# Layer 0's end, layer 1's degrees and layer 2's gates: part of the dilation moved, and two products put in column groups

## The chip, the core and the metric

The kernel runs on one core of one Trainium2 chip, in one launch. The metric is the device time of that launch in microseconds. TensorE multiplies matrices and writes to PSUM, VectorE and ScalarE do element-wise work and empty PSUM, GpSimd (POOL) computes a few powers and issues the stores to DRAM, SyncE (SP) issues the loads.

## The reference, cut to what matters

Four graph layers follow each other on `x` (16 x 1024 x 128, f32) with an adjacency matrix `adj` (16 x 1024 x 1024, zeros and ones) per batch. After each layer, `x = layernorm(x + layer(x))`.

Layer 0 is an attention: `h = x W^T + b`, `e = h A h^T` made symmetric, masked by `adj`, softmax along the rows, `h' = relu(att h)`, and one gate `c = sigmoid([x, h'] g)` that mixes `x` and `h'`.

Layer 1 first thins out the adjacency ("dilation"): row by row, every neighbour whose rank is a multiple of half the row's count is removed, from the row and from the column of the same number, and the next row sees what is left:

```python
sf = jnp.where(num > T_DIL, (num + K_DIL - 1) // K_DIL, 1)
rank = jnp.cumsum(nbi)
rm = row & (rank % sf == 0)
carry = carry.at[n].set(row & keep)
carry = carry.at[:, n].set(carry[:, n] & keep)
```

Then come three steps of `agg = (adj_d @ x) / deg; out = agg @ Wr + x @ Wx + b`, normed per row, relu and batch norm, where `deg` is the row sum of the thinned adjacency. Their outputs are joined and multiplied by `Wl`.

Layer 2 is an attention as in layer 0 with three gates in place of one: `i, f, o = sigmoid([x, h'] w)`, result `o * tanh(sigmoid(i h' + f x))`. Layer 3 is two graph convolutions with the normed adjacency.

## The kernel before, in words

A batch's adjacency is 1024 x 1024; it is kept as fp8 in SBUF (`Y[b]`, 8 tiles of 128 rows), four batches to one tile `Yq`. The phases are one after the other, each with its own pools: layer 0, the dilation, layer 1 (three steps over all batches), layers 2 and 3 together.

**Order of the work.** Each phase is written as Python generators, one per batch and stage, that `take_turns` (L803) runs round-robin: one stretch of each up to its `yield`. `in_turn` (L807) does it for the attention layers: while batch b is in `attention`, batch b+1 is in `before` and batch b-1 in `after`; at the end, the last `attention` runs with the last but one `after`, and then the last `after` (L825). This gives the order of the program. The build then places the instructions on each engine's queue; mostly in that order, but an instruction whose inputs, tile and PSUM bank are ready may be put ahead of one that comes earlier in the program. [...]

**Layer 0** (L884 to L995). `before` loads `adj` and turns it (L922), `attention` has eight stages of e (L723), mask and maximum (L958), exponent (L962) and product with h (L969). `after` takes relu, the gate, the mixture and the layer norm (`normed`, with a power on POOL, L744), and stores `x1` (L992). The gate goes through `gates` (L768 to L781), which holds the 32 gate columns as the stationary operand and puts the four quarters of the 1024 nodes into four column groups of TensorE:

```python
nc.tensor.matmul(p[32 * q:32 * q + 32, :], g, x[:, q * N // 4:(q + 1) * N // 4], ..., tile_position=(0, 32 * q))
```

ScalarE copies the result (L776), and two transposes (L779) turn it back. The PSUM pool `ps_h` of the layer has two banks, tag "h".

**Dilation** (L1002 to L1181). It works on blocks of 128 rows (k = 0 to 7) and two groups of eight batches (g), 16 steps in all. `prepare` (L1019) counts on TensorE (L1054, matmuls of 128 columns or one column) and puts counts and thresholds together on VectorE, for four batches at a time. `fixed_point` (L1069) evaluates six times which of the block's own entries are removed: `mid` on VectorE (L1085), eight one-column matmuls `pd` (L1088), then `ti` (L1092). `removal` (L1121) forms the ranks of a batch's rows (L1131, L1133), the kept entries (L1135) and the thinned rows and columns. Before the change, the phase begins with `prepare` of both groups, then the inverse roots of the degrees (L1169 to L1175), and then a loop: `fixed_point` of step i in turn with the removals of step i-1, after each of which `prepare` of step i+1 begins. The first pass of the loop has `fixed_point` alone.

**Layer 1, first step** (L1255 to L1378, L1352 on). For batch b, `first` computes the degrees: `degree_product` (L1255) multiplies the thinned adjacency with a 128 x 128 block of twos, 2 x 8 matmuls of 512 columns, of whose 128 equal rows one is used. ScalarE copies that row (L1357), a small transfer makes it 8 x 128 (L1359), VectorE takes the minimum and the inverse (L1360 to L1363), it goes to DRAM (L1364) and comes back to all partitions (L1349). Then follow the transposes of x (L758), and the product with the adjacency as two f32r parts, `hi` and `lo` (L1251, L1252, `lo` with one buffer), 64 matmuls of 512 columns (L1284). `out` (L1388 to L1404) multiplies with Wx and Wr, `keep` transposes, stores, and forms the product for the next step. The three are in turn for batches b+1, b and b-1. The order of the batches is 8 to 15, then 0 to 7; the thinned adjacency of the latter is loaded from DRAM (L1331).

**Layers 2 and 3** (L1455 on). `before` joins layer 1's outputs (L765) and prepares the attention; `attention` is as in layer 0 (L723, L1571 to L1590); `after` takes relu, the gates (L1596 to L1605), the mixture, norm, and the whole of layer 3, with its propagations (L1527). Its PSUM pool `ps_h` has two banks too. The gates before the change are, for each of eight blocks of nodes, two f32 matmuls with the nodes as the stationary operand and three moving columns (L1600, L1601).

Of the kernel before, what the change touches and what calls it, by code (L numbers as in the profile page):

```python
# [22 lines left out]
P = 128  # L23
# [5 lines left out]
GB = 8  # L29
# [610 lines left out]
def fast_kernel(ctx: ExitStack, tc: tile.TileContext, t: dict, out: bass.AP, flag: bass.AP):  # L640
# [166 lines left out]
    def in_turn(before, attention, after, ahead=1, state=None):  # L807
# [17 lines left out]
        take_turns([beside, after(state[B - 1], B - 1)])  # L825
# [55 lines left out]

    with ExitStack() as ph:

        early = ph.enter_context(tc.tile_pool(name="l0_early", bufs=1, reuse_waits="tile"))  # L884
# [110 lines left out]
        in_turn(before, attention, after)  # L995

    with ExitStack() as ph:
        sb = ph.enter_context(tc.tile_pool(name="dl_sb", bufs=2, reuse_waits="tile"))
        small = ph.enter_context(tc.tile_pool(name="dl_small", bufs=3, reuse_waits="tile"))
        ps_b = ph.enter_context(tc.tile_pool(name="dl_pb", bufs=2, space=PSUM, reuse_waits="tile"))
        ps_d = ph.enter_context(tc.tile_pool(name="dl_pd", bufs=1, space=PSUM, reuse_waits="tile"))
        ps_s = ph.enter_context(tc.tile_pool(name="dl_ps", bufs=3, space=PSUM, reuse_waits="tile"))  # L1010
        ps_c = ph.enter_context(tc.tile_pool(name="dl_pc", bufs=2, space=PSUM, reuse_waits="tile"))

        def words(v):
            return v.bitcast(I32)

        def per_member(v):
            return v[:, :, None].to_broadcast([P, v.shape[1], P])

        def prepare(st, k, g):  # L1019

            ks = slice(k * P, (k + 1) * P)
            st.with_last = k >= NT - 2
            st.sk = sb.tile([P, GB, P], F16, name="sk")
            st.v1m = small.tile([P, GB], F32, name="v1m")
            st.l1 = small.tile([P, GB], F32, name="l1")

            st.front = sb.tile([P, GB, P], BF16, name="front", bufs=3)
            if st.with_last:
                st.last = sb.tile([P, GB, P], FP8, name="last")
            for q in range(GB // QB):  # L1030
                qs = slice(q * QB, q * QB + QB)
                b0 = g * GB + q * QB
                gs = slice(b0, b0 + QB)
                Yg = Yq[b0 // QB]
                uY = sb.tile([P, QB, P], FP8, name="uY")
                nc.vector.tensor_tensor(words(uY), words(Yg[:, :, k, ks]),
                                        words(upper8)[:, None, :].to_broadcast([P, QB, P // 4]), op=OP.bitwise_and)
                front = st.front[:, qs, :]
                kf = [kb for kb in range(4) if kb != k]
                nc.vector.tensor_tensor(front, Yg[:, :, kf[0], ks], Yg[:, :, kf[1], ks], op=OP.add)  # L1040
                if k < 4:
                    nc.vector.tensor_tensor(front, front, Yg[:, :, kf[2], ks], op=OP.add)
                else:
                    back = sb.tile([P, QB, P], BF16, name="back")
                    nc.vector.tensor_tensor(back, Yg[:, :, kf[2], ks], Yg[:, :, kf[3], ks], op=OP.add)
                    nc.vector.tensor_tensor(front, front, back, op=OP.add)
                s0 = ps_b.tile([P, QB, P], F32, name="s0")
                for i in range(QB):
                    terms = [(Y[b0 + i][:, kb, ks], P if kb <= k else 1, step0 if kb == k else None)
                             for kb in range(4 if k >= 4 else 0, NT)]  # L1050
                    if k >= 4:
                        terms.insert(0, (front[:, i, :], P, None))
                    for j, (y, n, m) in enumerate(terms):
                        nc.tensor.matmul(s0[:, i, :n], y, twos[:, :n] if m is None else m,  # L1054
                                         start=(j == 0), stop=(j == len(terms) - 1))
                l1 = st.l1[:, qs]
                nc.vector.tensor_tensor(st.sk[:, qs, :], s0, uY, op=OP.mult)
                nc.vector.tensor_scalar(st.v1m[:, qs], s0[:, :, 0], 0.5, -1.0, op0=OP.mult, op1=OP.add)
                nc.vector.tensor_scalar(l1, s0[:, :, 0], -1.0, None, op0=OP.add)
                if not st.with_last:  # L1060

                    nc.vector.tensor_tensor(past[:, k, gs], l1, s0[:, :, P - 1], op=OP.subtract)
                nc.vector.tensor_add(st.v1m[:, qs], st.v1m[:, qs], off[:, k, gs])
                nc.vector.tensor_add(l1, l1, off[:, k, gs])
                if st.with_last:
                    nc.vector.tensor_tensor(st.last[:, qs, :], st.sk[:, qs, :], per_member(l1), op=OP.is_equal, saturate=False)
                yield

        def fixed_point(st, k, g):  # L1069

            ks = slice(k * P, (k + 1) * P)
# [90 lines left out]
        for s in steps[:G2]:  # L1162
            for _ in prepare(*s):
                pass
# [543 lines left out]
```

## Time and profile before

| what | us |
|---|---|
| three timed runs | 3050.39, 3050.43, 3054.73 |
| the profiled run, span of the core | 3049.5 |
| TensorE busy | 2825.3 (93%) |
| VectorE busy | 2325.2 (76%) |
| ScalarE busy | 2018.8 (66%) |
| L1261, degrees: 256 matmuls, one | 0.380 |
| L1600 and L1601, gates: 512 records, one | 0.252 |
| L774, layer 0's gates: 256 records, one | 0.391 |

Busy time of TensorE is modelled from the records, and matmuls overlap, so that the mean of one is more than what a stream of them takes per matmul; the distance between starts is the better measure. An f32 matmul has two records.

By stages: layer 0 lasts to about 725 us, the dilation to 1145, layer 1's first step to about 1540, its other two to about 1850, and layers 2 and 3 to the end. Granted clock, where a stretch shows it, is the share of TensorE's full clock.

### The profile page before, as it was taken

Reading aid. Unit: us, or ns where it says so; the run is one execution under the profiler, and the core shown is the slowest. Engines: PE = TensorE matmul, PEld = TensorE weight load, DVE = VectorE, ACT = ScalarE, POOL = GpSimd, SP = SyncE. Lnnn points to the kernel's source line nnn. Section 1 sums busy time; section 2 is a strip of 40 time slices with the busy share of each in tenths; the row PEclk is TensorE's granted clock in tenths of the full one; section 3 lists DMA queues with packets and bytes.
Section 4 is the critical chain, followed back from the end, with each engine's and each line's share of the span. In section 5 each row is a group of like instructions: output and inputs, shape, how many; then the busy total and the mean of one; then the engine's idle time right before and its main releaser. Section 6 shows DMA issues by size and latency. Waiting matters only on the chain.

```text
span 3049.5 us, 42855 instructions
## 1 busy us (share of the span) xinstructions
PE 2825.3 (93%) x15187; PEld 1794.2 (59%) x15250; DVE 2325.2 (76%) x5972; ACT 2018.8 (66%) x3425; POOL 315.2 (10%) x292
## 2 busy tenths in 40 slices
PE   7999999996999989999999987999999999999995
PEld 3444444443666657777788873556555555555554
DVE  7898889887999986666678785676766776777665
ACT  5877787773888886655555435666666666666653
POOL 0000000003000001111122231000000000000000
PEclk9999999997999999999999998999999999999997
DMA  5344344430000043223367692011112211111000
GB/s 162 131 159 152 132 138 159 152 118 29 2 2 2 2 158 107 88 91 120 122 231 251 227 336 76 35 63 59 66 57 71 73 57 56 56 56 56 21 14 22
DMA packets 123217, 297.97 MB, mean 98 GB/s; under 512 B 12656, under 2 KB 64624, under 8 KB 115824
## 3 DMA queue, kind: packets, MB, share of 16 engines
q1 hardware_dynamic: 102384, 211.13, 20.6%
q0 software_dynamic: 20608, 84.00, 7.7%
q8 instruction: 122, 2.00, 0.3%
q14 instruction: 103, 0.84, 0.1%
HBM read 211.04 MB, written 84.02 MB: 97 GB/s over the span
## 4 chain that ended last, share of the span: by engine, by line
PE 58%; DVE 21%; ACT 9%; DMA 5%; issue 5%; POOL 3%; SPq 0%; POOLq 0%; ACTq 0%; DVEq 0%
PE acc L1284 9%; PE pmm L723 8%; PE ph L1527 7%; PE acc L1590 6%; PE ph L765 6%; PE ph L758 4%; PE ph L1388 4%; DMA an<-in_adj 3%; ACT xn L798 3%; PE s L1131 2%; PE acc L969 2%; POOL ln_rstd L744 2%; PE ph L1513 2%; DVE mid L1085 2%; DVE ln_st L791 2%
## 5 line engine op out<-in xcount | busy, mean ns | idle before, releaser
L723 PE MATMUL pmm<-G,hT 128*128 128x512 f32 x1024 | 520.2, 630 | 1.9 <-DVE mx L1576 1.4
L723 PEld LDWEIGHTS pmm<-G,hT 128*128 128x128 f32 x1024 | 188.3, 201 | 174.2 <-issue 148.7
L798 ACT ACTIVATE xn<-xn,ln_nb,ln_rstd 128x128 f32<-128x128 f32 x512 | 206.6, 481 | 91.9 <-DVE ln_nb L796 91.9
L1590 PE MATMUL acc<-em,hs 128*128 128x512 f32 x512 | 256.0, 612 | 12.1 <-DVE hs L1587 10.5
L969 PE MATMUL acc<-em,hs 128*128 128x512 f32 x512 | 243.5, 599 | 18.2 <-DVE hs L966 16.8
L1284 PE MATMUL acc<-a,hi 128*128 128x512 f32 x768 | 242.0, 400 | 1.1 <-ACT hi L1251 0.9
L1284 PE MATMUL acc<-a,lo 128*128 128x512 f32 x768 | 241.2, 398 | 1.9 <-DVE lo L1252 1.9
L744 POOL TENSOR_TENSOR ln_rstd<-ln_rstd,mhalf 128x8 f32<-128x8 f32 x64 | 105.4, 1646 | 1324.2 <-DVE ln_rstd L741 1266.2
L1133 ACT ACTIVATE q<-s,negc 128x512 f16<-128x512 f32 x256 | 170.3, 696 | 58.2 <-DVE negc L1112 22.3
L915 ACT ACTIVATE ab<-an 128x1024 bf16<-128x1024 f32 x128 | 134.5, 1052 | 105.8 <-DMA an<-in_adj 66.6
L1131 PE MATMUL s<-step,carry 128*128 128x384 bf16 (+3 forms) x1034 | 197.6, 302 | 7.3 <-DVE carry L1101 3.2
L1576 DVE CUSTOM_DVE_ANT_0 em<-pmm,msk 128x1024 f32<-128x1024 f32 x128 | 156.0, 1219 | 54.7 <-PE pmm L723 51.9
L1145 ACT ACTIVATE carry<-pc,negone 128x512 fp8e4<-128x512 f32 x256 | 166.5, 698 | 35.7 <-PE pc L1144 26.3
L958 DVE CUSTOM_DVE_ANT_0 em<-pmm,msk 128x1024 f32<-128x1024 f32 x128 | 156.1, 1219 | 35.0 <-PE acc L969 30.5
L1571 ACT ACTIVATE msk<-A,nbig 128x1024 bf16<-128x1024 fp8e4 x128 | 146.0, 1141 | 50.2 <-DVE mx L1576 48.4
L1284 PEld LDWEIGHTS acc<-a,lo 128*128 128x128 f32 x768 | 142.9, 188 | 42.8 <-DVE lo L1252 9.5
L918 DVE SCALAR_TENSOR_TENSOR chk<-an 128x1024 fp8e4<-128x1024 f32 x128 | 156.3, 1221 | 14.0 <-DMA an<-in_adj 13.6
L1284 PEld LDWEIGHTS acc<-a,hi 128*128 128x128 f32 x768 | 141.7, 188 | 34.0 <-ACT hi L1251 1.4
L923 DVE TENSOR_SCALAR carry<-pt 128x1024 fp8e4<-128x1024 bf16 x128 | 155.7, 1217 | 6.2 <-PE pt L922 6.1
L969 PEld LDWEIGHTS acc<-em,hs 128*128 128x128 f32 x512 | 90.9, 190 | 113.9 <-issue 87.7
L1388 PE MATMUL ph<-Wx,hT 128*128 128x128 f32 x768 | 152.3, 281 | 4.9 <-DVE l2WT L709 3.2
L962 ACT ACTIVATE em<-em,nmx 128x1024 f32<-128x1024 f32 x128 | 146.9, 1147 | 12.3 <-DVE nmx L960 11.8
(285 smaller groups left out, 6448.6 us busy)
## 6 DMA issues: line engine op xcount, KB each, us to landing
an<-in_adj SPq DMA_DIRECT2D x128, 512.0 KB, 3.9
adj_d<-carry POOLq DMA_DIRECT2D x16, 1024.0 KB, 4.9
A<-dil_d SPq DMA_DIRECT2D x16, 1024.0 KB, 6.6
rdeg<-rdeg_d SPq DMA_DIRECT2D x32, 512.0 KB, 4.2
ag_d<-ag POOLq DMA_DIRECT2D x32, 512.0 KB, 5.5
ag<-ag_d SPq DMA_DIRECT2D x32, 512.0 KB, 6.3
A<-adj_d SPq DMA_DIRECT2D x16, 1024.0 KB, 4.8
xn<-in_x SPq DMA_DIRECT2D x16, 512.0 KB, 4.0
```

The source lines that it names most:

```text
L723: nc.tensor.matmul(p[:, h * 512:(h + 1) * 512], lhsT, rhs[:, h * 512:(h + 1) * 512], start=True, stop=True)
L744: nc.gpsimd.tensor_tensor(r, r, mhalf[:, :n], op=OP.pow)
L765: nc.tensor.matmul(p, W, x[:, c], start=(i == 0), stop=(i == len(pairs) - 1))
L798: nc.scalar.activation(r[:, i, :], r[:, i, :], AF.Identity, scale=rstd[:, i:i + 1], bias=nb[:, i:i + 1])
L969: nc.tensor.matmul(s.acc[:, c], hs, em[:, c], start=(jt == 0), stop=(jt == NT - 1))
L1131: nc.tensor.matmul(s[:, lo or 0:], y, twos if lo is None else step[:, :512 - lo], start=(j == 0), stop=(j == len(terms) - 1))
L1133: nc.scalar.activation(q[:, h * 512:(h + 1) * 512], s, AF.Abs, bias=st.negc[:, i:i + 1])
L1145: nc.scalar.activation(Y[b][:, hb, ks], pc, AF.Relu, bias=negone, saturate=False)
L1284: nc.tensor.matmul(acc, part[:, jt, :], pieces[h * NT // 2 + i][:, j, :], start=(jt == 0 and p == 0), stop=(jt == NT - 1 and p == 1))
L1388: nc.tensor.matmul(p[:, i * P:(i + 1) * P], x[:, j * P:(j + 1) * P], W, start=(n == 0), stop=(n == 1))
L1527: nc.tensor.matmul(p, part[:, jt, :], A[:, jt, c], start=(jt == 0 and i == 0), stop=(jt == NT - 1 and i == 1))
L1590: nc.tensor.matmul(s.acc[:, c], hs, em[:, c], start=(jt == 0), stop=(jt == NT - 1))
```

## The change

Three things are changed.

*The first counts.* `prepare`, `fixed_point`, `removal` and `removals` move out of the dilation's block to before layer 0, with their pools held in an object `dl`. Their lines are otherwise unchanged, except that PSUM tags come from `dl.tags`. `in_turn` takes one more stream, `tail`, that comes first in turn with the end of the last batches. Layer 0 passes `first_counts`: `prepare` and `fixed_point` of step 0. It closes the pool of layer 0's early tiles, which now lie on the right side of SBUF, and opens the dilation's pools for counts there; its PSUM is layer 0's `ps_h`, tag "h". The dilation's own block begins with `prepare` of step 1, and its loop with i = 1.

*The degrees.* `degree_product` has 32 matmuls with 32 columns of twos, each over a quarter of the nodes (256 columns), in four column groups of one PSUM bank; the row is copied in four pieces.

*The gates of layer 2.* They go through `gates`, with weights padded with zeros to 32 columns.

```diff
-        take_turns([beside, after(state[B - 1], B - 1)])
+        take_turns([iter(tail), beside, after(state[B - 1], B - 1)])
...
+    def first_counts(psum):
+        early_ctx.close()
+        dl.counts = dl.ctx.enter_context(tc.tile_pool(name="dl_counts", bufs=2, side="right", reuse_waits="tile"))
+        dl.small = dl.ctx.enter_context(tc.tile_pool(name="dl_small", bufs=3, side="right", reuse_waits="tile"))
+        dl.ps_b = dl.ps_d = psum
+        dl.tags = "h", "h"
+        yield from prepare(*steps[0])
+        yield from fixed_point(*steps[0])
...
-        early = ph.enter_context(tc.tile_pool(name="l0_early", bufs=1, reuse_waits="tile"))
+        early_ctx = ExitStack()
+        early = early_ctx.enter_context(tc.tile_pool(name="l0_early", bufs=1, side="right", reuse_waits="tile"))
...
-        in_turn(before, attention, after)
+        in_turn(before, attention, after, tail=first_counts(ps_h))
...
-        for s in steps[:G2]:
-            for _ in prepare(*s):
-                pass
+        for _ in prepare(*steps[1]):
+            pass
...
-        for i in range(len(steps) + 1):
+        for i in range(1, len(steps) + 1):
             streams = [fixed_point(*steps[i])] if i < len(steps) else []
-            if i:
-                streams.append(removals(steps[i - 1], steps[i - 1 + G2] if i - 1 + G2 < len(steps) else None))
+            streams.append(removals(steps[i - 1], steps[i - 1 + G2] if i - 1 + G2 < len(steps) else None))
...
-            self.gw = wts.tile([P, 2, 3], F32, name="l2gw")
+            self.gw = wts.tile([P, 2, 32], F32, name="l2gw")
+            nc.vector.memset(self.gw, 0.0)
...
-            for h in range(H2):
-                c = slice(h * 512, (h + 1) * 512)
-                acc = ps_a.tile([P, 512], F32, name="acc")
-                for jt in range(NT):
-                    nc.tensor.matmul(acc, twos[:, :P], A[:, jt, c], start=(jt == 0), stop=(jt == NT - 1))
-                yield acc, c
+            acc = ps_a.tile([P, 512], F32, name="acc")
+            for jt in range(NT):
+                for q in range(4):
+                    nc.tensor.matmul(acc[32 * q:32 * q + 32, :N // 4], twos[:, :32], A[:, jt, q * N // 4:(q + 1) * N // 4],
+                                     start=(jt == 0), stop=(jt == NT - 1), tile_position=(0, 32 * q))
+            for q in range(4):
+                yield acc[32 * q:32 * q + 1, :N // 4], slice(q * N // 4, (q + 1) * N // 4)
...
-                    nc.scalar.copy(row[:, c], acc[0:1, :])
+                    nc.scalar.copy(row[:, c], acc)
...
-            pg = ps_h.tile([P, NT, 3], F32, name="pg", tag="h")
-            for i in range(NT):
-                c = slice(i * P, (i + 1) * P)
-                nc.tensor.matmul(pg[:, i, :], s.xT[:, c], gw[:, 0, :], start=True, stop=False)
-                nc.tensor.matmul(pg[:, i, :], hpT[:, c], gw[:, 1, :], start=False, stop=True)
+            pg = gates(ps_h, wide("x3T")[:, :N // 4], (gw[:, 0, :], s.xT), (gw[:, 1, :], hpT))
             gt = small.tile([P, NT, 3], F32, name="gt")
-            nc.vector.tensor_add(gt, pg, gb[:, None, :].to_broadcast([P, NT, 3]))
+            nc.vector.tensor_add(gt.rearrange("p (q t) g -> p q t g", t=2), pg[:, :, :, :3],
+                                 gb[:, None, None, :].to_broadcast([P, 4, 2, 3]))
```

## The prediction

> **What bounds the kernel now.** I read the page's busy shares first (TensorE 93%, VectorE 76%, ScalarE 66%), then the chain that ended last in the three places that the change touches, then busy time by stretch there.
>
> In layer 1's first step, from the chain (start, us, what):
>
> ```profile
> 1201.44 3.57 PE ph L1388 x32
> 1205.01 1.77 PE ph L758 x16
> 1206.78 8.41 PE acc L1284 x36
> 1215.19 0.88 PE acc L1261 x4
> 1216.07 6.77 PE acc L1284 x28
> 1222.84 2.61 PE acc L1261 x12
> 1225.44 3.57 PE ph L1388 x32
> ```
>
> One batch takes 24.00 us and all of it is TensorE; the degree product (L1261, 16 matmuls of 512 columns) is 0.88 + 2.61 = 3.49 of it. The four that stand apart fill a hole: L1284 there waits for `lo` (L1252, 1.22 us), which has one buffer. From 1370 on the batch takes longer:
>
> ```profile
> 1395.13 3.57 PE ph L1388 x32
> 1398.70 0.89 PE ph L758 x8
> 1399.59 1.56 issue
> 1401.14 1.06 PE ph L758 x8
> ```
>
> The wait is a PSUM buffer that L1397 frees; L1397 stands on VectorE behind L1360, which waits for the small transfer of the degrees (2.4 us in the timeline).
>
> In layers 2 and 3 the batch is the distance between first propagations (L1527), from the chain:
>
> ```profile
> 2102.14 7.31 PE ph L1527 x32
> ...
> 2172.45 7.28 PE ph L1527 x32
> ...
> 2244.40 7.27 PE ph L1527 x32
> ```
>
> So 70.3 us, then 71.95. Busy time by stretch says why (us, PE, PEld, DVE, ACT, POOL, then granted clock, DMA share, GB/s):
>
> ```profile
> 2136.00:2138.00 2.00, 2.00 (x9) 1.07 (x8) 2.00 (x7) 1.05 (x1) 0.38 (x1) 1.00 0.28 115
> 2276.00:2278.00 2.00, 2.00 (x10) 1.84 (x10) 0.26 (x2) 0.22 (x1) 0.81 (x1) 0.53 0.85 344
> ```
>
> The gate matmuls (L1600, L1601: 32 records of three columns, 3.49 us) end at 2134 and at 2276. The second time the clock falls to half for some 3.4 us, and matmuls behind them take twice as long (L723 0.85 us each and not 0.43). That is 1.7 us lost, the difference of the two periods. By the trace it follows the gates in 11 of the 16 batches. TensorE is busy for 70.2 of 71.95 us in such a period.
>
> Between layer 0 and the dilation, from the stretches:
>
> ```profile
> 719.00:725.00 6.00, 5.77 (x69) 3.33 (x68) 0.62 (x3) 1.68 (x5) 0.00 (x0) 1.00 0.15 45
> 725.00:733.50 8.50, 0.66 (x6) 0.48 (x5) 6.25 (x23) 0.28 (x1) 1.64 (x1) 0.79 0.00 0
> 733.50:744.00 10.50, 2.62 (x64) 2.46 (x63) 10.45 (x42) 3.19 (x8) 0.94 (x2) 0.50 0.18 51
> 744.00:756.50 12.50, 2.24 (x48) 1.88 (x50) 9.79 (x22) 0.00 (x0) 0.00 (x0) 0.50 0.02 5
> ```
>
> VectorE carries the end of layer 0, then two `prepare`, then one `fixed_point` in a row; the first removal begins at 756.54. VectorE idles 5.4 + 2.2 + 0.1 + 2.7 = 10.4 us in it.
>
> The precedent for column groups is layer 0's own gates, in the timeline:
>
> ```profile
> 723.17 0.64 PE L774 MATMUL pq<-hpT,l0gw 128*32 128x256 f32 x8
> 723.88 0.37 ACT L776 COPY r<-pq 128x256 f32<-128x256 f32 x1 [0.89 <-PE pq L774]
> 724.30 0.44 PE L779 MATMUL pg<-identf,r 128*128 128x128 f32 x2 [0.23 <-ACT r L776]
> ```
>
> Eight records of 0.39 us each lie in 0.64 us: four start within 0.02 us, four more 0.24 us after them.
>
> **What the Trainium skill says.** "TensorE: Matmul & The Clock Gate", Part 3, says that matmuls with small outputs put in different column groups run side by side, 3 of them 2.38 times as fast; the lines above agree for f32. "TensorEngine Tiling (Array Packing)", Key Properties, says that a change of tiling mode drains TensorE; the trace prices it below. Part 1 of the first page says that the clock falls to half after a window of about 3.4 us without enough activity; the stretches agree, though here TensorE has a row of instructions all the while. The same page, in its architectural detail, says that VectorE and ScalarE take instructions strictly in order; L1397 behind L1360 agrees.
>
> **The change part by part.** The sum is against the profile's 3049.5 us; the three timed runs are 3050.4 to 3054.7, so nothing is corrected.
>
> *Degrees.* Removed: 16 matmuls at 0.217, 3.49 us per batch. Added: 32 of 256 columns by 32 outputs, in eight rounds of four. In layer 0 a gate group lengthens the distance between its neighbours from 0.43 to 1.09 us: 0.66 for two rounds, so 0.24 each and 0.18 for going in and out. An f32 record of 256 columns is 0.213 (half of 0.43), so a round has 0.027 on top; at one pass of bf16 it is 0.108 + 0.027 = 0.135. Eight rounds and 0.18 make 1.26 us. Bounds: 1.05 with no extra per round; 3.6 with no overlap (32 x 0.108 + 0.18), as the trace has no bf16 column group.
>
> Not all of 2.23 us is won. The hole before `lo` stays (0.9), and so does the 0.7 us of L1376 that L1388 must await after the second product. Per batch: 15.17 (L1284) + 0.9 + about 1.0 (what is left of the degrees, over L1376) + 3.57 + 1.77 = 22.4, so 1.6 saved in nine batches. In the last six the small transfer decides. Four copies of one row (128x256 takes 0.357, so 4 x 0.36 = 1.43) now all follow the last matmul, where one of 0.57 did: the transfer leaves 0.86 later against the product's end, which is itself 1.6 earlier. TensorE gains 1.6 and waits 0.86 more: 0.75 saved. The first batch, with nothing beside it, saves 2.23 less 0.86, about 1.5. Sum: 9 x 1.6 + 6 x 0.75 + 1.5 = 20. ScalarE's added 0.29 per batch costs nothing: it is busy 14.4 of 24 us. The one PSUM bank in place of two only helps. POOL's two transfers stay. Bounds: 0 (no overlap) and 47 (all 32 matmuls fit in the hole: 2.4 x 9, and with no late transfer 4 x 6, and 1.5).
>
> *Gates.* Removed: 32 records at 0.112, 3.49 us. Added: four rounds of 0.24 and 0.18, 1.14 us; a ScalarE copy of 0.36; two transposes at 0.11. TensorE saves 3.49 - 1.36 = 2.13 per batch, 34 in all. The transposes wait for the copy, and everything behind them on TensorE's queue with them, unless other work stands between; in layer 0 that is 0.2 to 0.4 us where it shows (the last line above). Two "h" buffers are held in turn instead of one for 3.5 us. I take 28. Bounds: 34, and a loss where the copy stands behind an Exp and a mask (1.13 + 0.19 + 1.15 + 0.36 = 2.8 us per batch). Then the clock: without 3.5 us of three-column matmuls I expect full clock in the 11 batches, 11 x 1.7 = 19. Bounds: 0 and 19. The copy's 6 us in sum lie beside TensorE (ScalarE is busy 48 of 72 us). The memset of the weights and the three weight DMAs that follow it on SP stand in layer 1's last batches, once, under 1 us; nothing measurable. Together 47.
>
> *First counts.* The work is the same: `prepare` 4.8 us of VectorE and six rounds of 2.1 us, of which 1.6 busy. It moves ahead of `after` of batch 15, into memory that the early tiles of layer 0 leave, and its PSUM becomes "h". VectorE can now fill its idle 5.4 us (waiting for the last gates), 1.8 us (for POOL's power, L744) and 2.7 us (for `pd`); before 719 there are 7 us more. Against this stand waits for the two "h" buffers that `after` also uses, and counts that stand ahead of `after`'s steps: its x1 transfer on POOL is later, but is read 400 us later. The second `prepare` stays on the way to the removals; the small dinv store on SP moves with it and is needed only in layer 3. I take 8 of 10.4. Bounds: 0 and 14.
>
> Sum: 20 + 47 + 8 = 75; 3050 - 75 = **2975 us**.
>
> **The rivals.** *Only what TensorE loses outright* (3013): the degrees win 10, as waits for `lo`, the row and the transfer take back the rest; the gates win 24 but the clock dips elsewhere, in the stretch around 2300 that dips already (0.50 there); the counts win 3. For it: a planner orders all this, and it reshuffles. Against: the periods of 70.3 and 72.0 show that TensorE's time is the batch's time. *All fits* (2937): degrees 47, gates and clock 53, counts 13 by being placed before 719. For it: the build already moves ready work ahead (L1170 runs at 688, though it stands behind `prepare`). *Column groups don't overlap here* (3042): weight loads for every matmul serialise them, the clock too stays; only the counts win 8. Against: layer 0. *Slower* (3071): the copy L776 of layer 2 is placed behind long ScalarE work and TensorE stands in order behind the transposes. It undoes the gates' part at 2.9 us per batch (47 / 16) and the whole at 4.7; at 6 the time is 3050 + 16 x 6 - 75 = 3071. Against: 0.2 to 0.4 us in layer 0, where ScalarE is as busy.
>
> **How the numbers follow.** Forecast 0.52, only TensorE's part 0.25, all fits 0.14, no overlap 0.04, slower 0.05. A measurement of this kernel tells 0.2% (6 us) from no change. Faster: the first three and half of the fourth, 0.93; within 0.2%: 0.02; slower 0.05. The forecast's own range is 2955 to 2995; to hold eight in ten it reaches over most of the first rival and to the edge of the second: 2940 to 3020.
>
> **What would show it.** Degrees: L1261 in about 1.2 us per batch, the period at 22.4 before 1370; wrong if L1261's records don't lie over each other, or the period stays at 24. Late degrees: the wait before L758 near 2.4 us; gone if they were placed before the second product. Gates: pq and pg in about 1.4 us of TensorE, the period at 68 to 69 us, granted clock near 1.00 just after the gates; wrong if a dip follows them still, or if TensorE idles for L776 by more than 1 us. Counts: first removal near 748, VectorE without its idle 5 us around 722.

## The result, and the profile after

| | us | ratio to the kernel before |
|---|---|---|
| kernel before | 3050.4 (3049.2 to 3054.7) | |
| changed kernel | 3022.8 (3018.4 to 3026.9) | 0.9907 [0.9889, 0.9924] |

The change is worth 28 us, 0.9%, where 75 were forecast (2975 us, with 2940 to 3020 as its range).

The page of the changed kernel, its first part and the shares of the chain:

```profile
PE 2746.2 (91%) x15220; PEld 1724.3 (57%) x15282; DVE 2328.2 (77%) x5973; ACT 2027.6 (67%) x3473; POOL 324.1 (11%) x292
...
PE 37%; DVE 22%; issue 21%; ACT 9%; DMA 6%; POOL 5%; POOLq 0%; SPq 0%; ACTq 0%; DVEq 0%
```

TensorE's busy time fell by 79 us (2825.3 to 2746.2). Only 28 of these reached the end. TensorE's share of the chain fell from 58% to 37%: in much of the program something else now ends last.

The two profiled runs (3049.5 and 3020.8) differ by 28.7 us. Start times of the same instructions divide it:

| stretch | before | after | difference |
|---|---|---|---|
| start to the first removal | 756.54 | 757.29 | +0.75 |
| first removal to the end of the dilation | 389.96 | 394.10 | +4.1 |
| layer 1's first step | 394.85 | 378.16 | -16.7 |
| its other steps, to the first propagation of layer 3 | 415.53 | 417.54 | +2.0 |
| first propagation to the end | 1092.65 | 1073.73 | -18.9 |

The counts gave nothing, the degrees 17 for 20, the gates 19 for 47. The first removal is the first product for the ranks (L1131 before, L1009 after); layer 1's first step ends with the first product of the second (L1388, L1406). The 4.1 us in the dilation aren't the change's (below).

**Degrees, the steady batches.** The chain of the changed kernel (start, us, what), to be held against the 24.00 us of before:

```profile
1213.23 7.96 PE acc L1302 x34
...
1221.21 1.24 DVE lo L1269
...
1222.49 6.80 PE acc L1302 x28
1229.29 0.44 PE acc L1277 x12
```

With 3.77 for L1406 and 1.77 for L758 a batch is 22.04 us. Only 12 of the 32 degree matmuls still take a place of their own. The other 20 lie in the hole before `lo`, where the four wide ones lay.

**Layers 2 and 3.** Busy time in two batches, from one first propagation to the next but one (us, PE, PEld, DVE, ACT, POOL, clock, DMA share, GB/s), of the kernel before:

```profile
2171.96:2315.84 143.88, 140.43 (x531) 84.62 (x529) 100.09 (x309) 96.17 (x187) 11.70 (x8) 0.95 0.17 59
```

and of the changed kernel, with the two microseconds after the gates of one batch:

```profile
2229.66:2370.69 141.03, 133.24 (x504) 76.02 (x502) 101.04 (x310) 96.38 (x189) 12.67 (x8) 0.98 0.17 60
...
2332.10:2334.10 2.00, 2.00 (x9) 0.97 (x8) 1.10 (x5) 1.09 (x2) 0.90 (x1) 1.00 0.76 258
```

TensorE has 3.6 us less to do per batch ((140.43 - 133.24) / 2), the clock no longer falls directly behind the gates, and yet a batch is only 1.4 us shorter here (1.1 over thirteen batches: 71.93 to 70.83). TensorE now idles 3.9 us per batch. What it waits for is in the chain of the changed kernel:

```profile
2264.87 3.19 ACT xn L798 x8
2268.05 0.12 ACT gt L1619
...
2268.43 0.68 DVE yn L1623
...
2269.16 3.70 PE ph L765 x8
```

The gate's tanh (L1619) stands on ScalarE behind the eight normalising activations of the batch before (L798). VectorE then takes `yn`, which frees an "h" buffer, and TensorE goes on.

The clock still falls once in every period, some 56 to 66 us behind its first propagation (3.4 us at half clock from 2286.1, for one). Before, that dip came in 7 of the first 13 periods. In these thirteen the time at half clock fell from 85 us to 44 in all.

### The profile page after: what moved, and what is told of

Read it like the earlier page. It is cut to its first block, busy times and chain, and to the rows that moved or that the text cites. A ratio compares the mean times of both kernels' runs of the same rounds, so it can differ in the third digit from the quotient of the medians.

```text
span 3020.8 us, 42966 instructions
## 1 busy us (share of the span) xinstructions
PE 2746.2 (91%) x15220; PEld 1724.3 (57%) x15282; DVE 2328.2 (77%) x5973; ACT 2027.6 (67%) x3473; POOL 324.1 (11%) x292
## 4 chain that ended last, share of the span: by engine, by line
PE 37%; DVE 22%; issue 21%; ACT 9%; DMA 6%; POOL 5%; POOLq 0%; SPq 0%; ACTq 0%; DVEq 0%
PE ph L1545 8%; PE acc L1302 7%; PE ph L765 5%; PE acc L1608 4%; DMA an<-in_adj 4%; PE pmm L723 3%; PE ph L1406 3%; POOL ln_rstd L744 3%; ACT xn L798 3%; DVE ln_st L791 3%; PE ph L758 3%; DVE em L1594 2%; PE ph L1531 2%; PE acc L1141 2%; ACT em L1134 2%
## 5 line engine op out<-in xcount | busy, mean ns | idle before, releaser
L723 PE MATMUL pmm<-G,hT 128*128 128x512 f32 x1024 | 507.7, 613 | 6.7 <-DVE mx L1594 6.5
L798 ACT ACTIVATE xn<-xn,ln_nb,ln_rstd 128x128 f32<-128x128 f32 x512 | 207.2, 482 | 128.8 <-DVE ln_nb L796 128.8
L723 PEld LDWEIGHTS pmm<-G,hT 128*128 128x128 f32 x1024 | 179.2, 193 | 174.6 <-issue 141.4
L744 POOL TENSOR_TENSOR ln_rstd<-ln_rstd,mhalf 128x8 f32<-128x8 f32 x64 | 112.9, 1764 | 1336.2 <-DVE ln_rstd L741 616.7
L1009 PE MATMUL s<-step,carry 128*128 128x384 bf16 (+3 forms) x1037 | 199.7, 305 | 7.7 <-DVE carry L979 3.2
L1090 DVE SCALAR_TENSOR_TENSOR chk<-an 128x1024 fp8e4<-128x1024 f32 x128 | 156.3, 1221 | 16.8 <-DMA an<-in_adj 16.3
L1406 PE MATMUL ph<-Wx,hT 128*128 128x128 f32 x768 | 154.7, 284 | 5.2 <-DVE l2WT L709 3.2
```

The costliest lines, as they stand in the source:

```text
L723: nc.tensor.matmul(p[:, h * 512:(h + 1) * 512], lhsT, rhs[:, h * 512:(h + 1) * 512], start=True, stop=True)
L744: nc.gpsimd.tensor_tensor(r, r, mhalf[:, :n], op=OP.pow)
L798: nc.scalar.activation(r[:, i, :], r[:, i, :], AF.Identity, scale=rstd[:, i:i + 1], bias=nb[:, i:i + 1])
L1009: nc.tensor.matmul(s[:, lo or 0:], y, twos if lo is None else step[:, :512 - lo], start=(j == 0), stop=(j == len(terms) - 1))
L1406: nc.tensor.matmul(p[:, i * P:(i + 1) * P], x[:, j * P:(j + 1) * P], W, start=(n == 0), stop=(n == 1))
```

## The experiments

All ratios are to the kernel before, timed beside the run on the same chip; 0.001 is 3.05 us. From set to set the kernel before took 3046.0 to 3050.9 us, so where runs of two sets are compared, the ratios decide.

### Each part by itself

The first kernel has the moved counts alone, the second the degrees, the third the gates, the fourth degrees and gates. The fourth, against the changed kernel (the dilation then begins as in the kernel before):

```diff
-        in_turn(before, attention, after, tail=first_counts(ps_h))
+        in_turn(before, attention, after)
```

The first, against the changed kernel, in the lines that the two other parts touch:

```diff
-            for jt in range(NT):
-                for q in range(4):
-                    nc.tensor.matmul(acc[32 * q:32 * q + 32, :N // 4], twos[:, :32], ..., tile_position=(0, 32 * q))
+            for h in range(H2):
+                ...
+                    nc.tensor.matmul(acc, twos[:, :P], A[:, jt, c], start=(jt == 0), stop=(jt == NT - 1))
...
-            pg = gates(ps_h, wide("x3T")[:, :N // 4], (gw[:, 0, :], s.xT), (gw[:, 1, :], hpT))
+                nc.tensor.matmul(pg[:, i, :], s.xT[:, c], gw[:, 0, :], start=True, stop=False)
+                nc.tensor.matmul(pg[:, i, :], hpT[:, c], gw[:, 1, :], start=False, stop=True)
```

> Only the first counts are moved; degrees and gates as before. Theory: the counts win nothing, because the inverse roots of the degrees on POOL (21.7 us) now stand on that queue ahead of batch 14's norm, so that VectorE, in order, holds layer 0's last attention by 11 us; the first removal starts within 1.5 us of where it did (756.5), and the whole is 3048 to 3056. Rival, the forecast's own step: the counts fill VectorE's holes, first removal near 748, the whole near 3042.

> Only the degrees are put in column groups. Theory, from the trace of the changed kernel: about 2 us less per batch in thirteen batches, of which some 6 are lost at the start of layer 1, where TensorE then waits for its first load and runs at half clock afterwards, and some 3 at the end of the step: 3033 to 3040. Rival: the late start belongs to the moved counts and not to the degrees; then 3024 to 3031.

> Only layer 2's gates are put in column groups. Theory: TensorE saves its 2 us per batch and its clock dips, but the batch becomes bound by the chain from the second propagation over VectorE, POOL and ScalarE to the gate's factors, so that about 1.1 us per batch is left: 3030 to 3036. Rival: the part alone gives what was forecast (2.95 us per batch), and it is the other two parts that spoil it through a different order: 3000 to 3008.

> The changed kernel without the moved counts: degrees and gates alone. Theory: the counts win nothing and cost some 5 us in the dilation's last steps (three stretches of half clock), so this is 3014 to 3020, a little faster than the changed kernel (3022.8). Rival: the counts do win about 8 us that something later hides, and this is near 3031.

| parts | us | ratio | in us |
|---|---|---|---|
| counts | 3056.7 | 1.0024 [1.0013, 1.0036] | +7 |
| degrees | 3030.3 | 0.9929 [0.9910, 0.9949] | -22 |
| gates | 3037.1 | 0.9956 [0.9941, 0.9971] | -13 |
| degrees and gates | 3017.6 | 0.9892 [0.9870, 0.9914] | -33 |

The parts add up: -22 - 13 is near the -33 measured, and +7 more gives the changed kernel. No part spoils another. The counts are a loss, the degrees are worth about what was forecast, and the gates less than a third. The gates and the counts miss the theory's range by 1 us. The degrees come 3 us under it and into the rival's, but the rival's reason doesn't hold: the late start of layer 1 is in this trace too, where no counts are moved (from the dilation's last thinned column to the first product with Wx 20.3 us, 14.9 before). Of the 7 us that the counts lose, the trace shows 1.5 in layer 0 and 4 in layer 1's first two batches (3 are left at the end of the step). There the first load of `x` leaves 1.2 us ahead of the dilation's end, in every trace with moved counts 1.0 to 1.2, and 5.7 in those without: SyncE's queue stands 7.3 us behind one of the dilation's last `keep`, presumably because a weight of layer 1 now lies in its memory. In this trace the small transfer beside these loads takes 7.1 us to land in place of 3.8, and TensorE waits 2.77 us for `ag`. Another 3.7 us in the dilation are clock, as follows.

These traces also settle the dilation's 4.1 us. The kernel with the gates alone has the same instructions on every engine as the kernel before until layer 1. From the first removal to the last thinned column, before, then with the gates alone:

```profile
756.54:1146.50 389.96, 366.22 (x4056) 238.89 (x4118) 365.51 (x1050) 315.63 (x515) 4.58 (x8) 0.99 0.09 34
```

```profile
758.33:1152.24 393.91, 369.93 (x4056) 241.25 (x4118) 365.98 (x1050) 316.40 (x515) 4.66 (x8) 0.98 0.09 33
```

The same work takes 3.95 us longer, and TensorE is busy 3.7 us longer at a lower clock. In the changed kernel three stretches of 3.4, 3.4 and 6.8 us at half clock (from 1050, 1078 and 1105) stand for it. The kernel with the minimum behind `lo` (below) has the changed kernel's dilation; in its trace there is no such stretch, and the dilation takes 390 us. So the 4.1 us are the execution's, not the change's.

### The counts: POOL's long power

The timeline of POOL in the kernel before (start, us, engine, line, operation; idle before it in brackets):

```profile
688.53 20.75 POOL L1170 TENSOR_TENSOR deg<-deg,mhalf 128x128 f32<-128x128 f32 x1
711.25 1.64 POOL L744 TENSOR_TENSOR ln_rstd<-ln_rstd,mhalf 128x8 f32<-128x8 f32 x1 [1.98 <-DVE ln_rstd L741]
```

and of the changed kernel, POOL and then VectorE:

```profile
697.22 21.73 POOL L1185 TENSOR_TENSOR deg<-deg,mhalf 128x128 f32<-128x128 f32 x1 [10.54 <-DVE nmx L1132]
718.94 1.63 POOL L744 TENSOR_TENSOR ln_rstd<-ln_rstd,mhalf 128x8 f32<-128x8 f32 x1
```

```profile
720.60 0.17 DVE L796 SCALAR_TENSOR_TENSOR ln_nb<-ln_mv,ln_rstd 128x8 f32<-128x8 f32 x1 [12.84 <-POOL ln_rstd L744]
```

The inverse roots of the degrees were on POOL before, too, at 688.5, and done at 709.3, 2 us ahead of batch 14's norm. Now they start at 697.2. Batch 14's power waits behind them, VectorE waits 12.84 us for that power, and everything behind it on VectorE waits as well, the last attentions first of all. From the last adjacency store of layer 0 to its last attention: 34.0 us before, 46.6 after. From there to the first removal: 34.6 before, 24.6 after. So the counts do win their 10 us, and 12.6 are lost ahead of them.

In both programs the power is written behind a `prepare` of the dilation, and the build puts it ahead, as its inputs are ready. Two kernels therefore hold it back by data. The first puts its input into a buffer of the removals:

```diff
+            if i == 3:
+                dg = sb.tile([P, N], FP8, name="keep").bitcast(F32)[:, :BT]
+                nc.vector.tensor_scalar(dg, deg, 1.0, 1.0, op0=OP.add, op1=OP.max)
+                nc.gpsimd.tensor_tensor(dinv, dg, mhalf[:, 0:1].to_broadcast([P, BT]), op=OP.pow)
+            if i == 6:
+                pt = ps_s.tile([BT, P], F32, name="pt", tag="s")
...
```

> The changed kernel (3022.8) with the inverse roots of the degrees kept back until the dilation's third step (their input goes through a buffer that the removals use). Theory: the counts do fill VectorE's holes by 10 us, but POOL's long power took it back; without it ahead of batch 14's norm, layer 0's last attention ends as before and the first removal 8 to 10 us earlier than before: 3011 to 3016. Rival: the counts themselves, placed among the last attentions, hold them up; then the last attention still ends about 10 us late, and this is 3020 to 3026.

Measured: 3033.5, ratio 0.9953 [0.9938, 0.9968]; slower than the changed kernel. It misses both ranges. The first removal does start at 745.97, 10 us earlier than before, as the theory had it. But then the dilation stands still, since `keep` has two buffers and POOL holds one:

```profile
841.22 0.75 DVE L1013 TENSOR_SCALAR keep<-q,wid 128x1024 fp8e4<-128x1024 f16 x1 [17.69 <-POOL deg L1193]
```

The second gives the power a tile of its own, tied to the third step by one column:

```diff
-                dg = sb.tile([P, N], FP8, name="keep").bitcast(F32)[:, :BT]
+                dg = sb.tile([P, BT], F32, name="dg", bufs=1)
+                nc.vector.tensor_copy(dg[:, 0:1], steps[3][0].v1m[:, 0:1])
```

> As the run before with the late power, but the power's input has a tile of its own, tied to the third step by a copy of one column, so that it holds no buffer that the removals need (the 20 us that the dilation then stood still). Theory: the 10 us that the counts win before the first removal now reach the end: 3009 to 3016, where the changed kernel has 3022.8. Rival: the dilation has no use for the earlier start, because its steps are bound by VectorE and by clock dips that vary from run to run; 3019 to 3025.

Measured: 3013.5, ratio 0.9881 [0.9860, 0.9901], inside the theory's range. By the ratios that is 8 us under the changed kernel, whose interval overlaps this one, so the trace has to tell. Its POOL:

```profile
713.59 1.66 POOL L744 TENSOR_TENSOR ln_rstd<-ln_rstd,mhalf 128x8 f32<-128x8 f32 x1 [20.71 <-DVE nmx L1132]
```

The long power comes at 800.48. From the last adjacency store to the first removal it is 57.5 us, where it was 68.6 before and 71.2 in the changed kernel: the counts are worth 11 us when nothing is lost ahead of them.

### The gates: what stands ahead of the tanh

The last norm of a batch is written after the gates of the next:

```diff
+            if ended:
+                finish(*ended.pop())
             yn = rows("yn", 2)
...
-            normed(small, s.xn)
-            nc.gpsimd.dma_start(nat(out[b]), s.xn)
+            ended.append((s, b))
```

> The changed kernel (3022.8) with the last norm of a batch written after the gates of the next, so that the gate's tanh stands ahead of the eight normalising activations on ScalarE. Theory: the gate's factors come some 5 us earlier, the two "h" buffers with them, and the period of layers 2 and 3 falls from 70.8 to 68 to 69 us: 2978 to 2998. Rival: the chain through VectorE and POOL (stats, power, mixture, next norm) bounds the batch wherever the tanh stands; the period stays within 0.5 us: 3015 to 3025.

Measured: 2999.3, 1 us over the theory's range, ratio 0.9849 [0.9827, 0.9871]. This kernel leaves out the norm and the store of batch 14, which its last lines never reach. So it was run again with both:

> The changed kernel (3022.8) with the last norm of each batch after the gates of the next, and those of the last two batches at the end (the earlier run left out the norm and the store of batch 14). Theory: period 68.7 us as there, 2992 to 3001. Rival: the norms at the end cost what the order won in the last batches: 3003 to 3010.

Measured: 3003.9, ratio 0.9856 [0.9841, 0.9871], 16 us under the changed kernel by the ratios; thirteen periods gain 27 us, as the theory said, and the last batches give 8 back, as the rival said. ScalarE in the kernel before, where the tanh stands ahead of L798 by itself:

```profile
2134.55 0.22 ACT L1604 ACTIVATE gt<-gt 128x24 f32<-128x24 f32 x1 [2.16 <-DVE gt L1603]
...
2138.10 3.17 ACT L798 ACTIVATE xn<-xn,ln_nb,ln_rstd 128x128 f32<-128x128 f32 x8
```

and in the changed kernel with the order changed:

```profile
2328.08 0.21 ACT L1625 ACTIVATE gt<-gt 128x24 f32<-128x24 f32 x1
2329.09 3.19 ACT L798 ACTIVATE xn<-xn,ln_nb,ln_rstd 128x128 f32<-128x128 f32 x8 [0.80 <-DVE ln_nb L796]
```

The tanh follows the end of the second propagation after 8.8 us (2319.3 to 2328.1) in place of 12.7 (2325.5 to 2338.2). The gate sum on VectorE comes after 7.6 us in both, and the gate's factors 3.5 us behind its start in place of 5.6: 2.1 us earlier, and the period is 2.1 us shorter. The edit moves the norm's statistics and its power along with L798, so their part in this isn't separated. Two batches take

```profile
2225.54:2363.14 137.60, 129.16 (x503) 73.88 (x501) 100.52 (x309) 96.13 (x189) 12.16 (x8) 1.00 0.18 62
```

so 68.8 us each, the 68 to 69 that the forecast named. In the kernel before, the gates took longer on TensorE, but needed no copy, and the build placed the tanh first. Is the order worth something without column groups? The same edit on the kernel before:

> The kernel before (3050.4) with only the order of the last norm changed as in the earlier run (the last norm of a batch after the gates of the next); its gates stay in rows of 32 three-column matmuls. Theory: before the change the batch is TensorE's time (70.2 of 71.9 us busy), so the order is worth little by itself: period 71 to 72.2, 3042 to 3056; the 2.1 us per batch that it won in the changed kernel are the gates' own gain, set free. Rival: the order is worth its 2 us per batch in any kernel: period near 69.8, 3015 to 3025.

Measured: 3054.5, ratio 1.0015 [1.0000, 1.0030], inside the theory's range. The mean of thirteen periods, in turn shorter and longer (67 to 75), is 71.3 us, and the last batches give that gain back. So of the four: before 71.9, order alone 71.3, gates alone 70.9, both 68.8. Neither is worth much without the other; together they save 3.2 us per batch.

The clock was asked for by itself: the gates of before, unchanged in form, with 32 columns in place of 3.

```diff
-            self.gw = wts.tile([P, 2, 3], F32, name="l2gw")
+            self.gw = wts.tile([P, 2, 32], F32, name="l2gw")
+            nc.vector.memset(self.gw, 0.0)
...
-            pg = ps_h.tile([P, NT, 3], F32, name="pg", tag="h")
+            pg = ps_h.tile([P, NT, 32], F32, name="pg", tag="h")
```

> The kernel before (3050.4), its gates unchanged in form but with 32 moving columns in place of 3 (29 of them zeros). It asks for the clock alone. Theory of the forecast: the dip comes of 3.5 us of three-column matmuls; with 32 columns the array is busier, the granted clock stays at 1.00 behind the gates and the longer period falls by 1.7 us in 11 batches: 3031 to 3040. Rival: the dip has another cause (an idle stretch before, or the weight loads), it stays, and the time is 3048 to 3058.

Measured: 3096.9, ratio 1.0168 [1.0150, 1.0187]; both theories missed the time. A matmul takes the same 0.11 us, but the build spreads every second batch's gates over 14 us, and that batch takes 79 to 82 us, for whatever reason. The clock can still be read, behind gates in one piece:

```profile
2287.50:2289.50 2.00, 2.00 (x6) 1.38 (x6) 0.26 (x2) 0.22 (x1) 1.56 (x1) 0.50 1.02 426
```

With 32 columns it falls behind 7 of the 8 rows of gates in one piece, and behind 1 of the 8 that are spread. In the kernel with the order alone it falls behind 4 of 6 rows spread over 11 us. So three columns are not the cause, and breaking the row up is no sure cure. What is shown is that in the changed kernel, with column groups, the clock is 1.00 in the 4 us behind the gates in all 16 batches.

The records of the clock tell more. In each of the traces, all changes of the granted clock lie on one grid of 3.413 us (within 0.002 us). In the five traces with the gates in rows there are 56 rows in one piece, the last batch left out. Behind 51 of them the clock falls, and there at least 2.24 us of the row lie within the step of the grid that ends with the fall; behind the other 5 it doesn't, and no step holds more than 2.22 us of the row. A row takes 3.63 us or more, with three columns as with 32, so where it begins on the grid decides; with column groups the products take 1.07 us. That the length of the row is the cause fits all this, but no run changes the length alone, and why a busy row counts as idle stays open.

### The degrees: the first batch and the last six

The start of layer 1 in the timeline of the changed kernel, TensorE, then VectorE:

```profile
1155.48 1.25 PE L758 MATMUL ph<-identf,n 128*128 128x128 f32 x8 [4.38 <-DMA n<-x_d]
...
1161.45 1.22 PE L1302 MATMUL acc<-a,lo 128*128 128x512 f32 x2 [3.67 <-DVE lo L1269]
```

```profile
1158.94 0.27 DVE L1378 TENSOR_REDUCE nodeg<-d 8x1 f32<-8x128 f16 x1 [7.69 <-DMA d<-row]
...
1160.25 1.15 DVE L1269 TENSOR_TENSOR lo<-n,hi 128x1024 fp32r<-128x1024 f32 x1
```

VectorE in the kernel before:

```profile
1150.27 1.22 DVE L1252 TENSOR_TENSOR lo<-n,hi 128x1024 fp32r<-128x1024 f32 x1 [3.91 <-ACT hi L1251]
1153.44 0.27 DVE L1360 TENSOR_REDUCE nodeg<-d 8x1 f32<-8x128 f16 x1 [1.94 <-DMA d<-row]
```

The first degrees take 1.06 us and not 3.47, but what follows isn't there: `n` is still on its way, and then `lo` stands behind the minimum, which waits for the small transfer. Before, `lo` stood ahead of it. That `n` is late comes with the moved counts (above). With the degrees alone it is there in time; TensorE then waits 3.32 us for `hi` and 4.93 for `lo`, and loses as much. With the two holes goes a stretch at half clock from 1156 to 1166. The Trainium skill ("TensorE: Matmul & The Clock Gate", Part 1) says that the clock falls after an idle window of some 3.4 us; holes of 4.38 and 3.67 us agree. From the dilation's last thinned column to the first product with Wx it is 14.9 us before, 20.5 after.

The first kernel makes the minimum and the inverse follow `lo`, in every batch:

```diff
+                nc.vector.tensor_copy(nodeg[:NT, b:b + 1], parts[1][:NT, 0, 0:1].bitcast(F32))
                 nc.vector.tensor_reduce(nodeg[:NT, b:b + 1], d16, AX.X, OP.min)
                 d8 = small.tile([NT, P], F32, name="d8", bufs=1)
+                nc.vector.tensor_copy(d8[:, 0:1], parts[1][:NT, 0, 0:1].bitcast(F32))
```

> The changed kernel (3022.8), the degrees' minimum and inverse made to follow the batch's own lo part on VectorE (two one-column copies tie them), so that no product waits behind the small transfer. Theory: the first batch of layer 1 loses its hole of some 4 to 5 us and the half clock after it (6 us), and the waits in the last batches shrink: 3008 to 3017. Rival: the inverse then comes late for the first half of the product, and each batch waits at its scaling instead: 3023 to 3040.

Measured: 3018.8, between the two ranges; the ratio, 0.9907 [0.9890, 0.9925], is the changed kernel's own. In its profile (3009.2) the step is 11 us shorter: the start is back to 16.3 us, four of the last five batches take about 22 in place of 24.4, and some batches before take up to 24.2, where the inverse now comes late. The timed runs (3010.95 to 3020.73) don't resolve this.

The second copies the row at once:

```diff
-                for acc, c in degree_product(st.A):
-                    nc.scalar.copy(row[:, c], acc)
+                nc.scalar.copy(row, degree_product(st.A))
...
-                nc.gpsimd.dma_start(d16, row)
+                nc.gpsimd.dma_start(d16, row.rearrange("(q r) n -> q r n", r=32)[:, 0, :])
```

> The changed kernel (3022.8), the four copies of the degrees' row put together: one copy of all 128 partitions (128x256), and the small transfer reads the four rows from partitions 0, 32, 64 and 96. Theory of the forecast: in the last six batches the transfer leaves 1.1 us earlier and the wait on it shrinks by as much, 0.9 to 1.1 us each; with the first batch 3015 to 3018. Rival: the wait is for VectorE's place in the queue and not for the copies; 3021 to 3025.

Measured: 3013.2, ratio 0.9878 [0.9858, 0.9898], under the theory's range. By the ratios it is 9 us under the changed kernel, whose interval overlaps a little; in the profiles the step is 15 us shorter. In all of the last six batches the wait before L758 is gone, and they take 22.04 us. The copy is 1.1 us shorter, but 2.4 are saved. The transfers show where the rest comes from. In the changed kernel, in batches of the first nine, then in the last six (issues, KB, median us to landing):

```profile
d<-row POOLq DMA_DIRECT2D x7, 2.0 KB, 1.5
```

```profile
d<-row POOLq DMA_DIRECT2D x6, 2.0 KB, 4.7
```

and the last with one copy:

```profile
d<-row POOLq DMA_DIRECT2D x6, 2.0 KB, 1.9
```

In the last batches the next adjacency is loaded (1 MB, L1349). With four copies the small transfer left at 1388.52, 0.30 us after that load (1388.22), and took 4.9 us to land. With one copy it left 0.82 us ahead of the load (1389.68 and 1390.50) and took 1.9. The form of its source differs as well (four partitions in place of one), so that the place ahead of the load isn't shown alone.

### Together

Late power, order of the norm, and the minimum behind `lo` in every batch:

> The changed kernel with the late power (own tile), the last norm after the next gates (the last two batches normed at the end), and the degrees' minimum behind lo. Theory: the three gains add, as they lie in different phases: 10 in layer 0 to the dilation, 11 in layer 1's first step, 25 to 30 in layers 2 and 3: 2970 to 2982. Rival: layer 1's part gives nothing to the end (its timed run was 3018.8, within the changed kernel's interval), and the other gains overlap: 2985 to 2995.

Measured: 2977.1, ratio 0.9760 [0.9737, 0.9783], inside the theory's range. The gains add. That they come to 73 us, near the 75 of the forecast, took three edits more than it counted on. With one copy on top:

> The combination of the run before (2977.1) with the degrees' row copied at once, as in the kernel with one copy. Theory: with the minimum tied behind lo nothing waits for the transfer any more, so the earlier transfer is worth at most 2 us: 2974 to 2979. Rival: the 9 us that one copy won in the changed kernel come on top, because ScalarE is freed for hi and the widened adjacency: 2966 to 2970.

Measured: 2977.1, ratio 0.9756 [0.9740, 0.9771]: nothing more, as the theory had it: with the tie to `lo` the earlier transfer has no wait left to take away. Last, one copy, with the tie to `lo` in the first batch alone:

```diff
+                if b != B // 2:
+                    inverse()
...
+                if b == B // 2:
+                    inverse(parts[1][:NT, 0, 0:1].bitcast(F32))
```

> Late power with its own tile, last norm after the next gates, one copy of the row, and the minimum tied behind lo in the first batch of layer 1 only. Theory: the tie is needed only where TensorE has nothing else (the first batch, 4 to 5 us) and costs 3 to 4 us in the batches where the inverse then comes late; so 2966 to 2972, against 2977.1 with the tie in every batch. Rival: the first batch's hole fills with another wait, 2974 to 2979.

Measured: 2963.8, ratio 0.9734 [0.9721, 0.9747], under both ranges, but the kernel before is 4.6 us faster in this set (3046.0) than beside the first 2977.1 (3050.7). It is 82 us under the kernel before and, by the ratios, 53 under the changed one. Layer 1's first step takes 356.8 us, where it took 394.85 before and 378.2 in the changed kernel.

## Why the prediction was wrong

*Degrees: the sum right, two of its terms wrong.* Forecast 20, measured 22 by time and 16 in the trace of that part alone. L1277 takes 1.06 us alone (1.26 forecast): eight rounds at 0.13, as the estimate of 0.135 had it. The period is 22.04 (22.4). The last batches save 1.0 each in place of 0.75. The step that failed is that the first batch, with nothing beside it, saves 1.5 us (2.23 less 0.86): with the degrees alone its first product with Wx comes 5.4 us later (20.3 us after the dilation in place of 14.9). The matmuls removed there were what filled the time until `hi` and `lo` came, and VectorE now has `lo` behind the minimum. The next batch takes 2.8 us of this back. The sum also had nothing for the end of the step, which takes 31.0 us from the last batch's product and not 28.1; why isn't shown.

*Gates: the step that failed is the 28 us of TensorE and the 19 of the clock as time of the batch.* Both came about on TensorE: 3.6 us less per batch, the clock at 1.00 behind the gates of all 16 batches. The prediction counted dips in 11 batches; in the 4 us behind the gates 14 of the 16 have one, three of them beginning 1 to 2 us late. The conclusion "TensorE's time is the batch's time" didn't hold. At 70.2 of 71.95 us TensorE had 1.7 us to spare, and the chain over VectorE, POOL and ScalarE, in the order that the build now gives it, takes 70.8. The forecast priced the copy L776 and looked for its wait at the transposes. It didn't follow the gate further: `gt` on VectorE, its tanh on ScalarE, and what stands ahead of that. From the start of the gate sum to the end of the gate's factors it took 2.8 to 4.1 us before and 5.6 after. The rival "slower" named ScalarE's queue, but ahead of the copy; it was ahead of the tanh. With that order changed the term measures 3.2 us per batch, where 47 / 16 = 2.9 was forecast; over the whole stage it is 38 us, as the last batches give some back.

*Counts: the step that failed is that their only costs are waits for "h" and a later x1 transfer.* The 8 us forecast are there (10 between the last attention and the first removal). What was missed is POOL's power of 21 us, and with it 12.6 us; that the first loads of layer 1 would leave later, for another 4 us, was not foreseen either. The prediction noted that it runs at 688, ahead of its place, and took this for a good sign. It didn't ask when it would run with the counts in the program (its input, L1184 on VectorE, now stands at 696.9), nor did it ask what comes next on POOL, batch 14's norm. That POOL, VectorE and ScalarE take their queues strictly in turn, as the Trainium skill says ("PSUM — Partial Sum Buffer", Engine vs sequencer instructions), is what the 12.84 us show for POOL and VectorE, and the tanh right behind L798 for ScalarE.

*The first rival* (3013) lies nearest, by luck for the most part. Its dips elsewhere did come, in every period where 7 of 13 had one, but the time at half clock still fell from 85 us to 44; the degrees didn't stop at 10, and the counts gave nothing and not 3. *No overlap* is excluded by L1277. Of the signs that the prediction named, those of TensorE came (1.06 us for the degrees, 22.04, clock 1.00, no wait for L776 above 1 us), and those of the batch didn't (68 to 69, first removal near 748).

## What to carry to other kernels

Before a saving on the busiest engine is counted as time, add up the next chain through the same batch: where the engine is busy for 98% of the period, another chain may be only 2% shorter. Follow every step that an edit makes later up to the instruction that frees a buffer for the busy engine, and at each queue on the way ask what stands ahead of it. Of a long operation that the build may place freely, ask where it lands after the edit; holding it back by data works, but not by a buffer that others need.

## What the runs showed that was not expected

- Four column groups of bf16 by fp8 matmuls, 32 columns by 256, lie over each other: 32 of them took 1.06 us, 0.13 for each four, where 16 of 512 columns took 3.47.
- A small transfer of 2 KB landed after 1.5 us in the first nine batches and after 4.7 in the last six, where a load of 1 MB left 0.3 us ahead of it.
- The same instructions of the dilation took 389.96 and 393.91 us in two executions. Clock dips come and go there, so that a difference of 4 us between two kernels in such a stretch is no evidence for either.
- Holes of 4.4 and 3.7 us on TensorE came with 10 us at half clock. The wide degrees had filled a part of that stretch, and without them the first product of layer 1 comes 5.4 us later.
- In every trace the granted clock changes only on a grid of 3.413 us. Whether 3.6 us of short matmuls are followed by half clock went by how much of them lay in one step of it: at least 2.24 us in 51 rows that were, at most 2.22 in 5 that were not.
